# Shift layer on Trainium2: tiles loaded by eight transfers over 128 partitions in place of four over 32, and each half tile stored after its own addition

## The chip, the cores and the metric

The kernel runs as one program on one core of a Trainium2 chip. The metric is device time in microseconds (us), the median of several executions. One further execution was taken with the hardware profiler; times inside the program come from that one. The engines are named as the profile names them: PE (matrix multiply), DVE (vector), ACT (scalar), POOL (GpSimd), SP (the engine that here only issues transfers). "SPq" and "ACTq" are rows for issuing a DMA transfer from SP or ACT.

## The reference, cut to what matters

The reference has four residual layers on `x` of shape (8, 384, 32, 32) in float32: a selective-scan (Mamba) layer, a deformable convolution, a second selective-scan layer with an MLP, and the shift layer. Only the last is touched:

```python
    def _L3_conv_ref(x, offset):               # offset: (48, 2), 48 positions of 8 channels each
        ...
        off_round = jnp.round(offset)
        off_int = off_round.astype(jnp.int32)
        disp = _displace(x.reshape(B, P, cpp, h, w), off_int).reshape(B, C, h, w)   # whole-pixel shift, zeros outside
        sub = offset - lax.stop_gradient(off_round)
        ...                                     # 5 x 5 Gaussian centred at the fractional rest, sum 1
        kw = jnp.repeat(kernel, cpp, axis=0)[:, None]
        out = lax.conv_general_dilated(disp, kw, ..., feature_group_count=C, ...)
        return out
    ...
    x = x + _L3_conv_ref(_gn(x), L3_conv_offset)     # _gn: group norm over 32 groups, no affine
```

A shift by whole pixels and a separable Gaussian are one banded 32 x 32 matrix over rows and one over columns, and all 8 channels of a position share them.

## The kernel before, in words

Layers 0 to 2 take the first 8566 us and are the same in both kernels. While layer 2 finishes, its result goes to DRAM twice: by samples, and as `x3s` with shape [384 channels, 32 rows, 8 images x 32 columns] (L612), so that one row of one channel is 1024 contiguous bytes that hold all 8 images.

The shift layer is built by `shift_parts`. It works in 12 tiles (`NM`). A tile `sxr` has 128 partitions, which are 4 positions (`IG`, index n) times 32 rows; each partition holds 8 channels (`CPP`, index k) x 8 images x 32 columns, 8 KB. So a tile is 1 MB. It is worked on in two chunks of half a tile, chunk 2m with channels k = 0 to 3 and chunk 2m + 1 with k = 4 to 7.

For each tile `load(m)` fills `sxr` from `x3s` (L1962), on SP. For each chunk c: `scale(c)` on POOL multiplies by the group norm's factor into `sxa` (L1980); `over_y` on PE applies the row matrix (L1990, L1992); `turn` on DVE transposes 32 x 32 blocks (L1996); `over_x` on PE applies the column matrix (L2002); `turn_back` on DVE transposes again (L2009); `add(c)` on POOL adds the result to `sxr` in place (L2014). After the second chunk of a tile the stores of the whole tile are written into the program: 32 of them (L2019), one for each channel of the tile, 32 KB each. The stores go in turn to the queues of ACT and SP; each consists of runs of 128 bytes, because the output lies by images.

`main` is a software pipeline with these steps in each turn i:

```python
            for i in range(-3, nch):
                for k, fn in ((3, scale), (2, over_y), (1, over_x), (2, turn), (1, turn_back), (0, add)):
                    if 0 <= i + k < nch:
                        fn(i + k)
                m = i // 2 + AHEAD
                if i % 2 and AHEAD <= m < NM:
                    load(m)
```

Five tiles (`AHEAD`) are loaded ahead of it; `load(m + 5)` is written behind the stores of tile m. `big` hands out the tiles' space from seven buffers in turn, and `done` gives one back. On POOL, `scale(i + 3)` stands ahead of `add(i)`.

The engines run their instructions in order. A scheduler places the waits between engines. For the transfers of SP and ACT it uses eight completion counters: a transfer is given one of the eight, and before it is issued its queue waits until the transfer that had that counter before has landed. Loads and stores of both queues share the eight.

Of the kernel before, what the change touches and what calls it, by code (L numbers as in the profile page):

```python
# [18 lines left out]
H = W = 32  # L19
# [22 lines left out]
CPP = 8  # L42
NP = C // CPP
IG = P // H
# [58 lines left out]
class Net:  # L103
# [1704 lines left out]
    def shift_parts(self, wp, p2, dap, big, done, src_of, srcs, dst):  # L1808
        nc, ins, nb = self.nc, self.ins, self.nb
# [3 lines left out]
        d = {}  # L1813
# [6 lines left out]
        def bc(name, *shape):  # L1820
            t = big(name)
            n = 1
            for k in shape:
                n *= k
            return t[:, :n]
# [131 lines left out]
        CH = NI * W // 2  # L1957
        def load(m):
            xr = d["xr", m] = bc(f"sxr{m}", NI, W).rearrange("p (i w) -> p i w", w=W)
            for n in range(IG):  # L1960
                c = (m * IG + n) * CPP
                nc.sync.dma_start(  # L1962
                    out=xr[n * H : (n + 1) * H].rearrange("p (k b) w -> p k (b w)", k=CPP),
                    in_=srcs[c : c + CPP].rearrange("k y b -> y k b"),
                )

        def table(c, t):
            m, h = divmod(c, 2)
# [4 lines left out]
        def piece(t, c):  # L1973
            return t[:, c % 2 * NI // 2 : (c % 2 + 1) * NI // 2].rearrange("p i w -> p (i w)")
# [36 lines left out]
        def add(c):  # L2011
            m = c // 2
            x = piece(d["xr", m], c)
            nc.gpsimd.tensor_tensor(x, x, d["zt", c], ALU.add)  # L2014
            if c % 2:
                done(f"sxr{m}")
                for k in range(CPP):
                    for n in range(IG):
                        (nc.sync if n % 2 else nc.scalar).dma_start(  # L2019
                            out=dst[:, (m * IG + n) * CPP + k, :].rearrange("b (y x) -> y b x", x=W),  # L2020
                            in_=d["xr", m][n * H : (n + 1) * H, k * nb : (k + 1) * nb, :],
                        )

        def main():
            nch = 2 * NM
# [8 lines that stand above are left out]
        return d, load_consts, kernels_a, kernels_b, stat_load, stat, norms, load, main  # L2034


# [100 lines left out]
```

## Time and profile before

| | |
|---|---|
| median of 3 executions | 8797.08 us (8791.13 to 8799.9) |
| profiled execution, its own time | 8793.49 us |
| its span, first to last instruction | 8791.7 us |
| mean granted PE clock | 0.909 |
| loads of the shift layer, L1962 | 48 of 256 KB, issued from 8566.2 to 8741.4 us |
| stores of the shift layer, L2019 | 192 on ACT's queue (8593.3 to 8772.2 us), 192 on SP's (8617.4 to 8789.0 us), 32 KB each |
| POOL in it | 24 scalings of 1912 ns, 24 additions of 2346 ns |

The times of rows are counted from the start of the span. The rows of a timeline give the start, the length from the first to the last of a group, the engine, the line, the operation, what is written and read, and how many. A wait row names who waited, for whom, how long in total, how often, and the longest. A DMA row of a window gives the packets, the megabytes and the time of the packets as a share of 16 engines' time in that window; it can pass 100% when packets overlap in an engine.

### The profile page before, as it was taken

The page shows a single profiled execution, that of the slowest core. Times are in us where ns is not written, and L with a number is a line of the kernel's source. Part 1 is how long each engine was busy: PE and PEld are TensorE (multiplying, and loading weights), DVE is VectorE, ACT ScalarE, POOL GpSimd, SP SyncE. Part 2 cuts the span into 40 slices and gives each one's busy share as a digit, 9 for nine tenths or more (in the row PEclk, how much of TensorE's full clock was granted, in tenths as well). Part 3 has the DMA queues.
Part 4 walks back from the last instruction along what each step waited for, and adds up shares of the span by engine and source line. Part 5 has one row for each costly group of instructions (what it writes and reads, how often), then busy time and mean ns, then how long its engine had stood idle before and what let it go on. Part 6 is the DMA issues. An engine that isn't in the chain of part 4 may idle for free. (4 is left out here: it accounts for less than half of the span.)

```text
span 8791.7 us, 91535 instructions
## 1 busy us (share of the span) xinstructions
PE 7389.6 (84%) x29688; PEld 3814.4 (43%) x29688; DVE 7510.6 (85%) x8477; ACT 5818.7 (66%) x9501; POOL 5571.8 (63%) x3383
## 2 busy tenths in 40 slices
PE   7888888788886899999999975788888888888886
PEld 2232233223222788788878861233333333333232
DVE  6999999999996788988898886898898988898872
ACT  6777777777774656665666556676777777776740
POOL 6999999999997000000000007999898989999954
PEclk8899899899887999999999997899889999999988
DMA  4555545555454654464446434566666656666646
GB/s 127 123 127 120 125 116 125 126 122 126 115 126 115 169 141 117 112 165 132 118 125 160 128 85 113 136 149 159 156 148 145 154 139 154 151 150 160 159 135 112
DMA packets 803572, 1179.30 MB, mean 134 GB/s; under 512 B 267042, under 2 KB 419650, under 8 KB 769288
## 3 DMA queue, kind: packets, MB, share of 16 engines
q1 hardware_dynamic: 743780, 1157.20, 53.7%
q10 hardware_dynamic: 57844, 10.06, 0.6%
q0 software_dynamic: 1456, 6.07, 0.2%
q8 instruction: 237, 3.88, 0.2%
q14 instruction: 255, 2.09, 0.1%
HBM read 984.11 MB, written 188.98 MB: 133 GB/s over the span
## 5 line engine op out<-in xcount | busy, mean ns | idle before, releaser
L539 POOL TENSOR_TENSOR db<-dub,bc 128x1024 f32<-128x1024 f32 x1536 | 3608.7, 2359 | 377.5 <-DVE hs L551 166.7
L531 ACT ACTIVATE da<-dtb,vec 128x512 f32<-128x512 f32 x3072 | 2122.1, 691 | 609.2 <-DVE hs L564 410.5
L551 DVE TENSOR_TENSOR_SCAN da<-da,db 128x1024 f32<-128x1024 f32 x960 | 2193.3, 2285 | 129.9 <-ACT da L531 86.9
L472 POOL TENSOR_TENSOR dt<-dt,sp_e 128x512 f32<-128x512 f32 x96 | 122.5, 1276 | 2473.1 <-DMA bc<-bcd 2468.8
L1792 PE MATMUL wacc<-fsm,fxk 128*128 128x195 f32 (+21 forms) x10624 | 1572.4, 306 | 132.5 <-DVE fsm L1755 69.7
L1792 PEld LDWEIGHTS wacc<-fsm,fxk 128*128 128x128 f32 x10624 | 1472.7, 195 | 269.1 <-DVE fsm L1755 141.3
L551 DVE TENSOR_TENSOR_SCAN hs<-da,db 128x1024 f32<-128x1024 f32 x576 | 1315.0, 2283 | 198.2 <-POOL db L524 86.2
L562 POOL TENSOR_TENSOR hs<-hs,bc 128x1024 f32<-128x1024 f32 x576 | 1358.0, 2358 | 33.8 <-ACT st L557 33.8
L564 DVE TENSOR_TENSOR hs<-da,bc 128x1024 f32<-128x1024 f32 x960 | 1175.5, 1224 | 127.9 <-PE y L574 78.6
L574 PE MATMUL y<-hs,cols 128*32 128x512 f32 x6144 | 975.4, 654 | 279.1 <-POOL hs L562 253.7
L1755 DVE TENSOR_TENSOR fsm<-fhy,fhx 128x585 f32<-128x585 f32 (+39 forms) x3136 | 1007.6, 383 | 92.9 <-PE wacc L1792 89.9
L1738 DVE TENSOR_TENSOR fxk<-fxt,fwk 128x1024 f32<-128x1024 f32 (+1 forms) x688 | 809.6, 1177 | 12.2 <-DMA fxt<-fxd 11.4
L1715 ACT ACTIVATE fhy<-fpyx,cell 128x416 f32<-128x416 f32 (+10 forms) x832 | 422.8, 580 | 374.7 <-DVE fsm L1755 374.6
L574 PEld LDWEIGHTS y<-hs,cols 128*32 128x32 f32 x6144 | 191.7, 114 | 1004.1 <-issue 516.1
L651 PE MATMUL ps_m<-hid,wm 128*128 128x512 f32 x1152 | 550.6, 633 | 61.8 <-ACT hid L646 27.8
L632 PE MATMUL ps_h<-t,wm 128*128 128x512 f32 x1152 | 531.1, 605 | 45.0 <-DVE sp_e L464 24.4
L1698 ACT ACTIVATE fhx<-fpyx,cell 128x352 f32<-128x352 f32 (+9 forms) x640 | 344.3, 609 | 237.0 <-DVE fsm L1755 222.8
L364 PE MATMUL ps_in<-xn,winr 128*128 128x512 f32 x576 | 326.8, 714 | 175.0 <-ACT xn L353 127.1
L651 PEld LDWEIGHTS ps_m<-hid,wm 128*128 128x128 f32 x1152 | 227.0, 203 | 394.7 <-issue 283.0
L632 PEld LDWEIGHTS ps_h<-t,wm 128*128 128x128 f32 x1152 | 216.1, 193 | 364.7 <-issue 273.4
L583 PE MATMUL ps_z<-xn,winr 128*128 128x512 f32 x576 | 303.0, 674 | 47.7 <-DVE sp_e L464 47.7
L1720 ACT ACTIVATE fhy<-fhy,cols 128x1184 f32<-128x1184 f32 (+8 forms) x208 | 307.4, 1478 | 6.8
(238 smaller groups left out, 9826.3 us busy)
## 6 DMA issues: line engine op xcount, KB each, us to landing
dtb<-dtd SPq DMA_DIRECT2D x768, 256.0 KB
dub<-dtd SPq DMA_DIRECT2D x768, 256.0 KB
fpyx<-fposd SPq DMA_DIRECT2D x104, 1024.0 KB
fxt<-fxd SPq DMA_DIRECT2D x96, 1024.0 KB
wm<-in_w SPq DMA_DIRECT2D x96, 768.0 KB
bc<-bcd SPq DMA_DIRECT2D x256, 256.0 KB
x<-x SPq DMA_DIRECT2D x73, 768.0 KB
dtd<-dt SPq DMA_DIRECT2D x192, 256.0 KB
```

What stands on the lines that cost most here:

```text
L531: nc.scalar.activation(da[:, i, :], s["dtb", j][:, k, :], AF.Exp, scale=na[:, j, n + i : n + i + 1])
L539: nc.gpsimd.tensor_tensor(db, du, s["bc"][p][:, 0], ALU.mult)
L551: nc.vector.tensor_tensor_scan(h1, da1, db1, 0.0, ALU.mult, ALU.add)
L562: nc.gpsimd.tensor_tensor(s["hs", m], s["hs", m], c, ALU.mult)
L564: nc.vector.tensor_tensor(hs_tile(s, m), s["da", m], c, ALU.mult)
L574: nc.tensor.matmul(s["y"][k * IP : (k + 1) * IP, :], sel, s["hs", p * NSUB + k][:, i, :], start=mlp and p == 0 and i == 0, stop=p == NQP - ...
L632: nc.tensor.matmul(ps, s["w1", q][:, k, f * P : (f + 1) * P], s["t"][:, k, :], start=(k == 0), stop=(k == G - 1))
L651: nc.tensor.matmul(ps, s["w2", q][:, f, o * P : (o + 1) * P], s["hid", q][:, f, :], start=(f == 0), stop=(f == 3))
L1715: nc.scalar.activation(hy[:, at : at + (yb - ya) * W], s["pyx", j][:, 0, ya * W : yb * W], AF.Abs, bias=bias)
L1738: nc.vector.tensor_tensor(t[:, :n], x, wk[:, j : j + 1, :].to_broadcast([P, n, P]), ALU.mult)
L1755: nc.vector.tensor_tensor(self.sub(sm, at, [(r * w, n), (w, r), (1, w)]), self.sub(hy, hy_at[by] + xa, [(r * W, n), (W, r), (1, w)]), self ...
L1792: nc.tensor.matmul(a[:, ya - 4 * o : yb - 4 * o, xa:xb], k, self.sub(sm, sm_at[by], [(w, yb - ya), (1, w)]), start=o not in s["open"], sto ...
```

## The change

A tile is loaded by eight transfers in place of four. Before, a transfer brought one position n: 32 partitions, each with eight rows of 1 KB. Now it brings one channel index k of all four positions: 128 partitions, each with one row of 1 KB, 128 KB. Its source in `x3s` is four blocks (the positions, 256 KB apart) of 32 consecutive rows. The 16 stores for channels k = 0 to 3 are written behind the addition of the first chunk, the 16 for k = 4 to 7 behind that of the second; before, all 32 stood behind the second. All else, the number of stores and bytes included, is as before.

```diff
         def load(m):
             xr = d["xr", m] = bc(f"sxr{m}", NI, W).rearrange("p (i w) -> p i w", w=W)
-            for n in range(IG):
-                c = (m * IG + n) * CPP
-                nc.sync.dma_start(
-                    out=xr[n * H : (n + 1) * H].rearrange("p (k b) w -> p k (b w)", k=CPP),
-                    in_=srcs[c : c + CPP].rearrange("k y b -> y k b"),
-                )
+            c = m * IG * CPP
+            src = srcs[c : c + IG * CPP].rearrange("(n k) y b -> k n y b", k=CPP)
+            for k in range(CPP):
+                nc.sync.dma_start(out=xr[:, k * nb : (k + 1) * nb].rearrange("p b w -> p (b w)"), in_=src[k])
 ...
             nc.gpsimd.tensor_tensor(x, x, d["zt", c], ALU.add)
             if c % 2:
                 done(f"sxr{m}")
-                for k in range(CPP):
-                    for n in range(IG):
-                        (nc.sync if n % 2 else nc.scalar).dma_start(
-                            out=dst[:, (m * IG + n) * CPP + k, :].rearrange("b (y x) -> y b x", x=W),
-                            in_=d["xr", m][n * H : (n + 1) * H, k * nb : (k + 1) * nb, :],
-                        )
+            for k in range(c % 2 * CPP // 2, (c % 2 + 1) * CPP // 2):
+                for n in range(IG):
+                    (nc.sync if n % 2 else nc.scalar).dma_start(
+                        out=dst[:, (m * IG + n) * CPP + k, :].rearrange("b (y x) -> y b x", x=W),
+                        in_=d["xr", m][n * H : (n + 1) * H, k * nb : (k + 1) * nb, :],
+                    )
```

## The prediction, made before the changed kernel ran

> **What bounds the shift layer now.** Only the last 226 us of the span are touched. I read the timeline of SP first, because every load and half of the stores go through it, then POOL's timeline, the chain of waits, and the DMA queues of two windows.
>
> ```profile
> 8566.23 50.72 SPq L1962 DMA_DIRECT2D sxr<-x3s  x20
> 8617.39 9.84 SPq L2019 DMA_DIRECT2D out<-sxr  x16
> 8627.27 5.71 SPq L1962 DMA_DIRECT2D sxr<-x3s  x4
> ...
> 8651.37 9.61 SPq L2019 DMA_DIRECT2D out<-sxr  x16
> 8661.02 8.17 SPq L1962 DMA_DIRECT2D sxr<-x3s  x4
> 8669.29 9.63 SPq L2019 DMA_DIRECT2D out<-sxr  x16
> ...
> 8741.98 47.47 SPq L2019 DMA_DIRECT2D out<-sxr  x80
> ```
>
> SP works in a beat: 16 stores (9.6 us), 4 loads (8.2 us), 17.9 us for a tile. It begins to store only at 8617 and ends last, at 8789.5, with 80 stores in a row. So SP sets the end. POOL doesn't:
>
> ```profile
> 8655.86 1.91 POOL L1980 TENSOR_TENSOR sxa<-sxr,stab 128x1024 f32<-128x1024 f32 x1 [9.95 <-DMA out<-sxr]
> 8657.73 2.35 POOL L2014 TENSOR_TENSOR sxr<-sxr,szt 128x1024 f32<-128x1024 f32 x1
> 8660.03 1.91 POOL L1980 TENSOR_TENSOR sxa<-sxr,stab 128x1024 f32<-128x1024 f32 x1
> 8661.90 2.35 POOL L2014 TENSOR_TENSOR sxr<-sxr,szt 128x1024 f32<-128x1024 f32 x1
> ```
>
> It has 8.4 us of work for a tile and then idles 9.5 to 10 us. The row blames a store, but a scaling reads what a load brings: tile 6 was issued from 8643.45 to 8651.3 and its scaling starts at 8655.86. (The two share a counter, so the name is the wrong one.) Loads reach POOL late although they stand five tiles ahead, because on SP they stand behind the stores of tile m.
>
> ```profile
> 8593.34 1.59 DMA out<-sxr
> 8594.95 3.05 DMA sxr<-x3s
> ```
>
> Issue to landing is 1.59 us for a store alone, 3.05 us for a 256 KB load. Last, the price of packets. Queue q1 is SP's; these are its rows in the window 8570 to 8582 us (loads alone) and 8776 to 8789 us (stores alone), and the page's totals:
>
> ```profile
> q1 hardware_dynamic: 2483, 2.40, 113.0%
> ...
> q1 hardware_dynamic: 7089, 0.86, 41.0%
> ...
> DMA packets 803572, 1179.30 MB, mean 134 GB/s; under 512 B 267042, under 2 KB 419650, under 8 KB 769288
> q1 hardware_dynamic: 743780, 1157.20, 53.7%
> q10 hardware_dynamic: 57844, 10.06, 0.6%
> ```
>
> A load's 1 KB packet takes 1.13 x 16 x 12 us / 2483 = 87 ns there, 200 GB/s in all. A store's 128 B packet takes 0.41 x 16 x 13 us / 7089 = 12 ns. In the trace's packet records the 1 KB packets have a lower quartile of 46 ns, and from 8627 to 8742 us a mean of 65 ns.
>
> **The change, part by part.** The built order of the changed program keeps POOL, PE, DVE and ACT as they were, instruction for instruction. SP gets 96 loads for 48 and the same 192 stores: 24 issues for a tile instead of 20. The step is about 0.5 us an issue (16 stores in 9.6 us, SP's issue row 449 ns), so 2 us more for a tile. One load is moved past stores: the first of tile 5 now stands ahead of tile 0's on SP.
>
> *Stores by halves.* I cost this at nothing. ACT's first store already goes at 8593.34, when the first addition (8590.96 + 2.35) ends, and the second addition starts only at 8600: each store waits for its own half already. And SP's stores run tiles behind the additions (the first at 8617 for an addition done at 8593). That lag is the cover; if it were gone, a half tile's POOL time, 4.3 us, would be gained once. A loss by it could come only through the counters, below.
>
> *The loads: on how many DMA engines?* This decides everything. Every shift transfer of the trace runs on 16 engines. [...] a transfer's engines are the largest number up to 16 that divides the outermost dimension (not of size 1) of both access patterns[...]. Each engine used sends one 4-byte packet at the end, so the trace can be asked: the rule, summed over all issues (18 rows give 9 engines, 50 give 10, 98 give 14), yields 56,600 on SP's queue and 3,706 on ACT's; the packet records hold exactly 56,600 and 3,706 (the few loads of 4-byte rows counted in; 16 for every transfer would be 57,064 and 3,716). But in each of these both patterns have suitable outer sizes. The new load has 128 partitions on one side and, in the built program, [4 positions, 32 rows, 256] on the other, for the positions aren't adjacent. By the rule that is 4 engines. By the nearest row (all present loads) it is 16, and 128 KB would be 8 packets to an engine, some 0.4 us. [...] I take the rule, since it missed none of 60,306 packets.
>
> Price of one load, L, by packet: 32 x 46 ns = 1.47 us if the four engines never meet; 32 x 87 ns = 2.8 us if two always share. [...] I take the stage's mean of 65 ns, L = 2.08 us; both ends stay in the range. Eight loads of a tile then need 16.6 us on the same four engines, where the four loads take some 5 us (1 MB at 200 GB/s) on sixteen.
>
> *Opening.* The built order gives the loads of tiles 0 to 4 (and the first of tile 5) all eight counters in strict turn, with no store between; today ACT's first store waits only for tile 0's load. Now SP's first store, its 42nd transfer, waits for tile 4's third load, the 35th, and ACT's for the 34th. First load packet at 8568.8 (packet records): 8568.8 + 35 x 2.08 + 0.5 landing = 8642 for SP's first store (now 8617). [...] lands at 8568.8 + 41 x 2.08 + 0.5 = 8654.6. SP's fifth store waits for it: 8655, and 12 stores x 0.5 later, 8661, tile 0 is stored (now 8627.3). Lost: 34 us. POOL's early scalings (tile 4's now at 8619.9) slip too, but are ahead of this.
>
> *Beat.* With a tile's first load issued at t, load j lands at t + 0.9 + 0.5 + jL: 1.4 us is the 3.05 of a load less its 16 packets (1.4) with a little rounding. Loads 6 to 8 wait for counters of loads 1 to 3, the next tile's first stores for loads 4 and 5, and the fifth store for the first, which stands behind all eight loads: t + 1.4 + 16.6 + 0.3. Then 12 stores: 24.3 us for 17.9. ACT waits with it, having handed counters to these loads. POOL's 8.4 us and ACT's 16 x 0.5 us fit within. Seven beats, less the one load already counted: 170 - 2 = 168 us, where SP now takes 114.7 us (8627.3 to 8742.0) and 9.5 for tile 7's stores, a fifth of its last row.
>
> *Tail.* From there 4 tiles x 16 stores remain, 64 x 0.5 = 32 us, and 2 us to the end. Sum: 8661 + 168 + 32 + 2 = 8863, against a span of 8791.7: +71 us. The profiled execution took 8793.49, 1.8 over its span and 3.6 under the median of 8797.08; I add the difference to the median: 8868 us.
>
> **Ends.** With 46 ns (and 1.5 us a beat for ACT's stores, which the mean of 65 ns holds already: half of 16 x 16 x 12 ns): store 0 ends at 8637, beat 21, 7 x 21 - 1.5, tail 34: 8817, +25, so 8822. With 87 ns: 8690, beat 30.1, 7 x 30.1 - 2.8, tail 34: 8932, +140, so 8937.
>
> **Rivals.**
> *Sixteen engines after all (faster).* Place: SP's queue in the beat. Eight loads of 128 partitions land 2 us after issue, and nothing waits but the issuing: 192 stores + 56 loads at 0.5 us = 124 us from 8594 (first addition), some 10 us of leftover waits and 2 us for the end: 8730, -62 us, 8735. For it: [...] the exact count of 4-byte packets never tried an outer 4 against 128. [...] The point of decision: with L = 1 us (8 engines) the same sum gives opening 8617, beat 17.2, end about 8770; it meets the present span near L = 1.15, seven engines.
> *Four engines that don't meet.* The end of 46 ns, 8822. For it: [...] 46 ns is the median of the stage. [...]
> *Neither.* The loads keep their 200 GB/s, and only 4 issues x 0.5 us are added for a tile, 14 us over seven beats, taken back by earlier first halves: near 8800.
>
> **Chances.** About 0.2% (18 us) is what this measurement can tell from no change. Four engines meeting in part: 0.52 (8840 to 8960); four engines not meeting: 0.26 (8800 to 8840); sixteen: 0.13; neither: 0.06; worse than 8960: 0.03. Slower by over 0.2% (above 8815): 0.79; within: 0.07; faster: 0.14. The range 8800 to 8960 leaves out sixteen engines and the worst, and about half of "neither": a little under 0.2. Nearly all of the chance is on one side.
>
> **What would show it.** Right: q1's packets fall by 384 to 743,396 (96 loads x 4 end packets for 48 x 16); with sixteen engines they rise to 744,548. SP's first store near 8642; the beat 21 to 30 us; in the opening a DMA share near a quarter with 50 to 90 GB/s, where it is full with 200. Waits of POOL at L1978 grow. Wrong, if the loads' window shows over 200 GB/s, SP's first store comes before 8600 and its beat is 12 to 13 us.

## The result, and the profile after

The changed kernel takes 8818.76 us (median of 10 executions, 8816.32 to 8824.0) where the kernel before takes 8795.81 us (10 executions in turn with it, 8787.18 to 8799.9). The ratio is 1.0028, 95% interval 1.002 to 1.0037: slower by 23 us. The forecast was 8868 us: the direction and the main mechanism (four engines) hold, but the loss is a third of the forecast one, and it lies where the rival "four engines that don't meet" put it (8822). The profiled execution took 8821.17 us over a span of 8819.4 us, at a granted clock of 0.908 against 0.909 before, so the clock plays no part.

The timeline of SP, after (start, length, what it issued):

```profile
8567.25 56.55 SPq L1963 DMA_DIRECT2D sxr<-x3s  x41
8623.91 13.47 SPq L2017 DMA_DIRECT2D out<-sxr  x16
8637.42 6.18 SPq L1963 DMA_DIRECT2D sxr<-x3s  x7
...
8657.17 7.49 SPq L1963 DMA_DIRECT2D sxr<-x3s  x8
8666.19 11.71 SPq L2017 DMA_DIRECT2D out<-sxr  x16
8677.95 7.79 SPq L1963 DMA_DIRECT2D sxr<-x3s  x8
...
8771.97 45.20 SPq L2017 DMA_DIRECT2D out<-sxr  x80
```

SP begins to store at 8623.9 (before: 8617.4), its beat is 20.8 to 21.7 us (before: 17.9), and it still ends last. Against the rows of before, the two spans differ by 27.7 us. Tile 0 is stored 10.1 us later (8637.4 for 8627.3; 1.0 us of it, because the stage starts that much later in this execution). From there to the last row (six beats and the loads of a seventh) it takes 134.6 us where it took 114.7: 19.9 us. From the last row to the end it is 2.3 us shorter.

SP's queue in the window 8570 to 8582 us (loads alone), then 8804 to 8817 us (stores alone), then over the whole page:

```profile
q1 hardware_dynamic: 1063, 1.06, 26.4%
...
q1 hardware_dynamic: 7237, 0.87, 41.8%
...
q1 hardware_dynamic: 743396, 1157.20, 53.2%
```

SP's queue has 743,396 packets, the number that the prediction gave for four engines. The loads fill 26.4% of sixteen engines, that is about four (25% would be exact), and move 89 GB/s in place of 200. A packet takes 0.264 x 16 x 12 us / 1063 = 47.7 ns there. In the packet records the 1 KB packets have a median of 46 ns and a mean of 48.1 ns from 8627 to 8742 us, where before had 65.

The chain of work that ended last shows the opening load by load (start, length):

```profile
8585.75 1.38 SPq L1963
8587.18 1.38 SPq L1963
...
8595.64 1.82 SPq L1963
8597.50 1.38 SPq L1963
```

Eight rows stand from 8585.75 up to 8597.50, each one load: 11.75 us, 1.47 us a load, which is 32 packets of 46 ns. The counters do not hold SP here. The load issued at 8575.50 landed at 8583.95 by the counter's own record, and the next load with its counter is issued only at 8587.18; from 8576 to 8622 us SP has no wait for a DMA. It is the issue itself that lasts 1.3 to 1.8 us, where before has 0.30 to 0.45 once its opening is under way. So the pace is that of the four engines, and SP's issuing is held to it; how it is held, the records do not tell. POOL (its timeline, and its waits: us in total, times, longest) runs at that pace too:

```profile
8594.39 1.91 POOL L1978 TENSOR_TENSOR sxa<-sxr,stab 128x1024 f32<-128x1024 f32 x1 [3.96 <-DMA sxr<-x3s]
8596.26 2.34 POOL L2012 TENSOR_TENSOR sxr<-sxr,szt 128x1024 f32<-128x1024 f32 x1
8600.27 1.91 POOL L1978 TENSOR_TENSOR sxa<-sxr,stab 128x1024 f32<-128x1024 f32 x1 [1.66 <-DMA sxr<-x3s]
...
POOL sxa L1978 <- DMA sxr<-x3s: 78.9, 13, 11.1
```

A scaling starts every 5.88 us, that is four loads of 1.47 us: half a tile. In before, the profile put POOL's waits at this line down to stores (74.1 us), which the prediction argued to be the wrong name. Here it puts 78.9 us down to loads and 25.5 to stores.

### The profile page after: what moved, and what is told of

Same layout as the page of the kernel before. It is cut to its first block, busy times and chain, and to the rows that moved or that the text cites. A ratio compares the mean times of both kernels' runs of the same rounds, so it can differ in the third digit from the quotient of the medians.

```text
span 8819.4 us, 91611 instructions
## 1 busy us (share of the span) xinstructions
PE 7399.1 (84%) x29688; PEld 3819.8 (43%) x29688; DVE 7503.8 (85%) x8477; ACT 5817.8 (66%) x9501; POOL 5572.0 (63%) x3383
## 3 DMA queue, kind: packets, MB, share of 16 engines
q1 hardware_dynamic: 743396, 1157.20, 53.2%
## 5 line engine op out<-in xcount | busy, mean ns | idle before, releaser
L651 PE MATMUL ps_m<-hid,wm 128*128 128x512 f32 x1152 | 550.9, 633 | 61.7 <-ACT hid L646 27.7
L583 PE MATMUL ps_z<-xn,winr 128*128 128x512 f32 x576 | 302.9, 674 | 47.7 <-DVE sp_e L464 47.7
```

The source lines that it names most:

```text
L651: nc.tensor.matmul(ps, s["w2", q][:, f, o * P : (o + 1) * P], s["hid", q][:, f, :], start=(f == 0), stop=(f == 3))
```

## The experiments

Theory F: the loss is the four engines, 8 x 1.47 us of loads for a tile ahead of the stores on the same engines. Rival I: it is the added issues (20 in the opening, 4 in a beat, 0.5 us each). Rival S: it is the stores by halves, through the order of the counters. All ratios are to the kernel before, on the same chip.

**One half of the change at a time.** The first kernel takes the new `load` and keeps the old stores:

```diff
-            for n in range(IG):
-                nc.sync.dma_start(out=xr[n * H : (n + 1) * H]..., in_=srcs[c : c + CPP]...)
+            for k in range(CPP):
+                nc.sync.dma_start(out=xr[:, k * nb : (k + 1) * nb]..., in_=src[k])
```

> The eight loads over 128 partitions alone; the 32 stores of a tile stay behind the second addition, as before. Theory F (four engines): a load of 128 KB runs on four DMA engines, 32 packets x 46 ns = 1.47 us of them, eight of them 11.8 us of a tile's beat, and this makes the whole loss: slower by 20 to 28 us (ratio 1.0023 to 1.0032), beat of SP near 21 us, first store of SP near 8624. Rival I (issues: 20 more in the opening, 4 more in a beat, 0.5 us each) expects the same here. Rival S (it is the stores by halves, which change whose counter waits for whom): no change, beat 17.9 us.

Measured: 8819.5 us, ratio 1.0028 (1.0018 to 1.0039), q1's packets 743,396. SP's timeline:

```profile
8567.78 56.32 SPq L1963 DMA_DIRECT2D sxr<-x3s  x41
8624.21 13.45 SPq L2017 DMA_DIRECT2D out<-sxr  x16
8637.70 6.20 SPq L1963 DMA_DIRECT2D sxr<-x3s  x7
```

It is the changed kernel over again, row for row within 1.2 us. The second kernel keeps the old `load` and takes the new stores:

```diff
             if c % 2:
                 done(f"sxr{m}")
-                for k in range(CPP):
+            for k in range(c % 2 * CPP // 2, (c % 2 + 1) * CPP // 2):
```

> The stores by halves alone; the four loads over 32 partitions as before. Theory F: each store already waited for its own half only, and SP's stores run tiles behind: within 5 us of before (ratio 0.9994 to 1.0006), beat 17.9 us. Rival I: the same. Rival S: slower by 15 to 25 us. A third way: the halves shorten the loop that holds the beat today (load landing, scaling, addition, ACT's stores, next load), and the gain was hidden in the changed kernel by the loads: faster by some us.

Measured: 8792.72 us, ratio 1.0001 (0.9992 to 1.0009), with the rows of before. So the loads make the whole loss, and the halves make nothing either way. S falls; F and I remain.

**The same issues and bytes on sixteen engines.** Each load takes one position and half of its channels:

```diff
-            for k in range(CPP):
-                nc.sync.dma_start(out=xr[:, k * nb : (k + 1) * nb]..., in_=src[k])
+            for k in range(0, CPP, CPP // 2):
+                for n in range(IG):
+                    c = (m * IG + n) * CPP + k
+                    nc.sync.dma_start(out=xr[n * H : (n + 1) * H, k * nb : (k + CPP // 2) * nb]...,
+                                      in_=srcs[c : c + CPP // 2].rearrange("k y b -> y k b"))
```

> As the changed kernel, but each of the eight loads of 128 KB takes one position (32 partitions, outermost dimension 32) and half of its channels: as many issues of as many bytes, on sixteen engines. Theory F: the loss goes; a load is 8 packets an engine, 0.4 to 0.7 us, so SP's beat is no longer set by them: not slower than before, ratio 0.993 to 1.000, q1's packets 744,548. Rival I (issues): as the changed kernel, ratio 1.0028. If the price were the 32 partitions and not the engines, the opening would still move 200 GB/s.

Measured: 8794.65 us, ratio 1.0003 (0.9995 to 1.0011), q1's packets 744,548. The loss is gone with as many issues as the changed kernel has: rival I falls. Why there is no gain either is looked at two experiments on.

**128 partitions, with the source in one, eight or two runs.** In three kernels only the choice of source rows differs from the changed kernel, so the order of all instructions and the counter of every transfer are those of the changed kernel, by the trace. (The rows come from other channels than the tables belong to, so these kernels leave out the right assignment, as the expectations say.) First, 128 rows that lie together:

```diff
-            src = srcs[c : c + IG * CPP].rearrange("(n k) y b -> k n y b", k=CPP)
+            src = srcs[c : c + IG * CPP].rearrange("(k n) y b -> k (n y) b", k=CPP)
```

> As the changed kernel, but each load reads 128 rows that lie next to each other in x3s (channels are assigned to positions in another order than the tables and stores have, so the output is a permuted mixture): 128 partitions, 128 KB, eight issues, and the source merges into one dimension of 128. Theory F: sixteen engines; L falls from 1.47 us to some 0.4 to 0.6 us, the opening's window shows over 200 GB/s [...], and the time is the forecast of sixteen engines, 8735, ratio 0.992 to 0.996. Rival I: ratio 1.0028. q1's packets 744,548 under F.

Measured: 8734.3 us, ratio 0.9934 (0.9921 to 0.9948), q1's packets 744,548. Then eight runs of 16 rows:

```diff
-            src = srcs[c : c + IG * CPP].rearrange("(n k) y b -> k n y b", k=CPP)
+            src = srcs[c : c + IG * CPP].rearrange("c (h y) b -> (c h) y b", h=2)
...
-                nc.sync.dma_start(out=xr[:, k * nb : (k + 1) * nb]..., in_=src[k])
+                nc.sync.dma_start(out=xr[:, k * nb : (k + 1) * nb]..., in_=src[k : k + 50 : 7])
```

> As the changed kernel in the same order, but each load reads eight runs of 16 rows of x3s, so the outermost dimension is 8 (the output is a mixture of rows; some rows are read twice and some not at all). Theory F: L = 16 x 46 ns = 0.74 us; by the prediction's sum the first store of SP comes at 8568.8 + 26 + 0.5 = 8595, tile 0 is stored at 8606, beat 1.4 + 5.9 + 0.3 + 6 + 1.5 = 15.1 us, end 8606 + 105 + 34 = 8745: ratio 0.993 to 0.996, between the changed kernel and the run on sixteen engines. q1's packets 743,396 + 384 = 743,780. Rival I: 1.0028. [...]

Measured: 8752.98 us, ratio 0.9955 (0.994 to 0.9971), q1's packets 743,780. Last, two runs of 64 rows:

```diff
-            src = srcs[c : c + IG * CPP].rearrange("(n k) y b -> k n y b", k=CPP)
+            src = srcs[c : c + IG * CPP].rearrange("(n k j) y b -> k n (j y) b", n=2, j=2)
```

> As the changed kernel, instruction for instruction in the same order, but each load of 128 KB reads two runs of 64 rows of x3s (channels assigned to positions in another order than the tables and stores have: the output is a permuted mixture), so the outermost dimension is 2. Theory F (engines = the outermost dimension, 46 ns a packet): L = 64 x 46 ns = 2.94 us. By the prediction's own sum with this L: SP's first store 8568.8 + 35 x 2.94 + 0.5 = 8672, tile 0 stored at 8696, beat 1.4 + 23.5 + 0.3 + 6 + 1.5 = 32.7 us, end 8696 + 7 x 32.7 - 3 + 34 = 8956: ratio 1.018. q1's packets 743,396 - 192 = 743,204. Rival I (issues): as the changed kernel, 1.0028. If the loss were the jumps between runs in DRAM, two long runs would be cheaper than four.

Measured: 8958.81 us, ratio 1.0191 (1.0175 to 1.0206), q1's packets 743,204. The loads' window, 8570 to 8582 us, for sixteen, eight and two engines in turn (packets, MB, share of sixteen engines):

```profile
q1 hardware_dynamic: 3455, 3.15, 84.7%
```

```profile
q1 hardware_dynamic: 2209, 2.13, 54.1%
```

```profile
q1 hardware_dynamic: 534, 0.54, 13.5%
```

The shares of the last two stand near eight and two engines of sixteen (50 and 12.5% would be exact), and a packet takes about the same in all three: share x 16 x 12 us / packets is 47.1, 47.0 and 48.5 ns, with the 4-byte packets counted in. In the packet records the 1 KB packets alone have a median of 46 ns in each, and means of 52, 49 and 49. It is not the number of runs in DRAM that costs: two runs cost most (ratio 1.0191) and eight (0.9955) cost less than four (1.0028). Beside the changed kernel's 26.4%, this is F's dose and answer:

| engines | L by 46 ns | span forecast by the prediction's sum | span measured | ratio |
|---|---|---|---|---|
| 2 | 2.94 us | 8956 | 8956.9 | 1.0191 |
| 4 (changed kernel) | 1.47 us | 8817 | 8819.4 | 1.0028 |
| 8 | 0.74 us | 8745 | 8751.4 | 0.9955 |
| 16 | 0.37 us, less than an issue | 8730 (its rival's sum, by issues) | 8732.5 | 0.9934 |

With sixteen engines the loads no longer set the pace: 41 loads take 20.64 us, one per 0.5 us, which is SP issuing.

```profile
8565.19 20.64 SPq L1963 DMA_DIRECT2D sxr<-x3s  x41
8591.76 8.98 SPq L2017 DMA_DIRECT2D out<-sxr  x16
8600.79 3.31 SPq L1963 DMA_DIRECT2D sxr<-x3s  x7
```

**Why sixteen engines over 32 partitions gain nothing.** That kernel and the one with adjacent rows have the same issues, bytes and engines, and lie 60 us apart. SP's waits, first of the kernel with 32 partitions, then of that with adjacent rows:

```profile
SPq L2020 <- DMA out<-sxr: 41.2, 27, 4.3
SPq L1963 <- DMA out<-sxr: 31.4, 17, 14.0
```

```profile
SPq L2017 <- DMA out<-sxr: 11.3, 16, 2.3
...
SPq L1963 <- DMA out<-sxr: 1.8, 4, 0.6
```

With 32 partitions all of the 31.4 us stand in the opening, where loads wait for counters that ACT's stores hold (one of these waits 14.0 us, 17.2 in before); with adjacent rows it is 1.8 us. In the beat of the 32-partition kernel, from 8621 to 8745 us, SP's loads don't wait, but its stores do: 33.6 us for stores and 12.5 for loads.

The trace names the counter of each transfer, and the two kernels hand the counters out differently. With 32 partitions SP's third store of a tile needs the counter of one of ACT's stores two tiles on; that store needs its addition, which on POOL stands behind the scaling of the tile loaded just before; and SP's next loads stand behind its stores. One turn reads: scaling of tile 5 at 8636.0 us, addition for tile 3 done at 8640.3, SP's third store of tile 1 at 8642.3, loads of tile 6 from 8649.6, their scaling at 8654.2. In before a load of tile m + 5 itself needs the counter of one of ACT's stores of tile m + 3, and from 8617 to 8741 us such loads wait 41.7 us. Either way this is a loop over one tile: load landing, scaling, addition, ACT's stores, next load. With adjacent rows (and in the changed kernel) the counters come from ACT's stores that are one or two tiles older, so the loop reaches further back. The loads' window also differs, 215 GB/s at 80 ns for a 1 KB packet against 263 GB/s at 52 ns (means of the packet records). The runs do not separate the two, so how much of the 60 us is the counters and how much the packets stays open.

**The loads off SP.** If before's beat is that loop, loads with other counters break it. The kernel before, with

```diff
-                nc.sync.dma_start(
+                nc.gpsimd.dma_start(
...
-                m = i // 2 + AHEAD
+                m = i // 2 + AHEAD - 1
```

> The kernel before with its four loads of 256 KB issued by POOL in place of SP, and from tile 5 on one half beat later in the order (load m + 5 behind the additions of tile m + 1, so that POOL does not wait for stores just issued). The reading of before: the beat of 17.9 us is a loop through the counters that loads share with ACT's stores (load landing, scaling, addition, ACT's stores, next load), and nothing in it is full: POOL has 8.4 us of work, SP 16 x 0.5. With counters of their own the loads leave the loop: beat 12 to 13 us, set by POOL (8.4 + 4 issues x 0.75 us, as the issues at L1222 cost), end some 40 to 60 us earlier: ratio 0.993 to 0.996. [...] Second rival: issuing and waiting on POOL take what is gained: 0.999 to 1.003.

(What the expectation calls half a beat is one tile in the order.) Measured: 8742.61 us, ratio 0.9944 (0.993 to 0.9957), the fastest of the kernels here that leave nothing of the computation out. POOL's timeline:

```profile
8630.08 2.34 POOL L1962 DMA_DIRECT2D sxr<-x3s  x4
8632.43 1.92 POOL L1980 TENSOR_TENSOR sxa<-sxr,stab 128x1024 f32<-128x1024 f32 x1
8634.30 2.35 POOL L2014 TENSOR_TENSOR sxr<-sxr,szt 128x1024 f32<-128x1024 f32 x1
8636.61 1.91 POOL L1980 TENSOR_TENSOR sxa<-sxr,stab 128x1024 f32<-128x1024 f32 x1
8638.48 2.34 POOL L2014 TENSOR_TENSOR sxr<-sxr,szt 128x1024 f32<-128x1024 f32 x1
8640.77 2.34 POOL L1962 DMA_DIRECT2D sxr<-x3s  x4
```

SP's timeline now has stores alone:

```profile
8604.03 134.36 SPq L2019 DMA_DIRECT2D out<-sxr  x192
```

POOL's beat is 10.7 us, without a gap: 8.4 us of work and four issues of 0.59 us. The 9.5 to 10 us of idling per tile that before showed are gone, and PE, too, is busy all the time from 8600 to 8712 us. The beat no longer sets the end: the last addition ends at 8719.6 us, and SP issues its stores, 0.70 us each, until 8738.4. A control moves the order alone:

> The kernel before with only the order moved: load m + 5 behind the additions of tile m + 1, all loads on SP. It tells what of the gain with loads on POOL is the order. On SP the load then stands behind one tile's stores more, so it comes later for scaling: the loop load, scaling, addition, stores is as long, ratio 0.999 to 1.006. If the order were the gain: 0.994 to 0.996.

Measured: 8790.88 us, ratio 0.9999 (0.999 to 1.0007). So the gain is the other queue, not the later place in the order. That queue has its own counters, it takes the loads out from behind SP's stores, and it moves larger packets (below); the runs do not separate these three.

**The changed kernel's loads on POOL**, by the same two edits made to it:

> The changed kernel with its eight loads of 128 KB over 128 partitions issued by POOL, the same half beat later. Theory F with the same rule on POOL's queue: the loads leave SP's order, [...] 17.9 us a tile, so near before (ratio 0.998 to 1.002), and its opening loads at under 90 GB/s. If the rule does not hold on POOL's queue (16 engines), the time is as of the four loads on POOL or a little above (8 issues): 0.993 to 0.997. Rival I: 1.00 or slower by POOL's 8 issues of 0.75 us: POOL 14.4 us a tile, still under 17.9.

Measured: 8762.84 us, ratio 0.9968 (0.9956 to 0.998). It is the second outcome: on POOL's queue the outermost dimension of 4 does not leave this pattern with four engines. (By the author's estimate these would have carried, for a tile, 8 x 1.47 us of loads and 8192 x 12 ns / 16 = 6.1 us of stores, 17.9 us.) The loads' window:

```profile
q0 software_dynamic: 2031, 1.92, 96.4%
```

The loads now keep all sixteen engines busy, with the very access pattern that SP's queue runs on four. They move 160 GB/s, less than the 215 of the 32-partition loads on POOL. Its stage has a beat of 13.7 us, which is POOL's 8.4 us and eight issues of 0.68, less small overlaps.

**Three tries to improve on it.** The loads of tiles 0 to 4 back on SP, the others on POOL (`(nc.sync if m < AHEAD else nc.gpsimd)`):

> The kernel before with the loads of tiles 0 to 4 on SP as before and those of tiles 5 to 11 on POOL, half a beat later in the order. In the run with all loads on POOL the beat is 10.7 us, but the opening has 20 issues on POOL ahead of the first scaling, and the first addition starts at 8601.7 in place of 8591. Theory: with the opening back on SP the first addition returns to 8591, the beat stays 10.7 us, and the time falls by a further 8 to 11 us: ratio 0.9925 to 0.994. Rival: the opening's loads wait for counters of ACT's stores as before (SP's first store at 8617), SP then runs tiles behind and its 16 x 0.5 us in a beat of 10.7 leave it 2.7 us to catch up: no gain over all loads on POOL, 0.994 to 0.996.

Measured: 8750.72 us, ratio 0.9953 (0.9939 to 0.9966). The first addition is back at 8591.3, but the rival was right. SP's timeline and waits:

```profile
8566.51 55.12 SPq L1962 DMA_DIRECT2D sxr<-x3s  x20
8621.73 124.58 SPq L2019 DMA_DIRECT2D out<-sxr  x192
...
SPq L1962 <- DMA out<-sxr: 39.5, 7, 17.2
```

The opening's loads stand 39.5 us on counters that ACT's stores hold, SP starts to store at 8621.7, and its 192 stores, 0.65 us each now, set the end. The same with the stores by halves:

> The same with the changed kernel's stores by halves. The prediction costed the halves at nothing because SP ran tiles behind the additions, and said that without this cover a half tile's POOL time, 4.3 us, is gained once. Where SP keeps up with the additions, the end comes up to 4 us earlier than in the run with whole tiles (ratio 0.0002 to 0.0005 lower). If SP still lags, the two are equal. If the halves cost by the counters, it is slower.

Measured: 8749.37 us, ratio 0.9952 (0.9938 to 0.9966): equal, since SP still lags (it starts at 8620.4). What the halves give where SP keeps up with the additions was therefore not tried alone. Last, four tiles ahead, eight opening loads on SP and eight on POOL, stores by halves:

> Four loads of 256 KB over 32 partitions (sixteen engines) for each tile: tiles 0 and 1 by SP, which takes eight issues and so each counter once, all others by POOL, two of them ahead of the first scaling; four tiles ahead in place of five; stores by halves. Against the run with all loads on POOL (20 issues ahead of the first scaling, first addition 8601.7, SP's first store 8604): POOL issues 8 loads, 4.7 us from 8567, before the tables it waits for anyway (8579), so the first addition is back at 8591, beat 10.7 us as there: 10 us earlier, and the halves give up to 4 us at the end where SP keeps up: span near 8728, ratio 0.992 to 0.9935. Rival: SP's and ACT's stores are no longer ahead of time to spare (16 x 0.65 us = 10.4 in a beat of 10.7), and what the opening gives is lost in their queues: 0.994 to 0.9955.

Measured: 8746.94 us, ratio 0.9947 (0.9934 to 0.9961): a miss, and not told apart from all loads on POOL. POOL's timeline shows what failed in the opening:

```profile
8571.06 4.68 POOL L1962 DMA_DIRECT2D sxr<-x3s  x8 [91.92 <-DVE smv L1903]
8589.63 3.78 POOL L1980 TENSOR_TENSOR sxa<-sxr,stab 128x1024 f32<-128x1024 f32 x2 [13.89 <-DMA sxr<-x3s]
```

The loads of tiles 2 and 3, issued by POOL at once, share the engines with those of tile 0, whose scaling waits for its load to 8589.6 in place of 8579 (some 4 us of it, because the stage starts that much later in this execution). Later, a load with one tile less of lead lands just too late: seven of the scalings wait 1.3 to 2.8 us for it. The stores' queues, the place that the expectation's rival named, end last: SP's 192 stores, 0.73 us each, run from 8605.3 to 8745.3 us, where the last addition ends at 8733.7.

## Why the prediction was right and wrong, point by point

- *SP sets the end.* Right: the issue of its last store ends at 8817.2, of a span of 8819.4.
- *Stores by halves cost nothing, because SP lags.* Right on the cost: ratio 1.0001 for the halves alone. That the lag is the reason was not tried alone.
- *Four DMA engines, by the outermost dimension of both patterns.* Right. The nearest row of the trace (all loads on sixteen) would have given a gain of 62 us; the rule, borne out by the count of 4-byte packets, decided the sign. In before, sixteen for each transfer would be 57,064 on SP's queue. The records hold 56,600: 464 fewer, which is what 9, 12, 10 and 14 packets make for its transfers of 18, 24, 50 and 98 rows (44, 2, 22 and 8 of them), the largest divisors up to 16. The loads with an outermost 2, 4, 8 and 128 bear it out on SP's queue: 743,204, 743,396, 743,780 and 744,548 packets, which is 2, 4, 8 and 16 of 4 bytes a load, and 13.5, 26.4, 54.1 and 84.7% of sixteen engines. In the changed kernel the load issued at 8575.50 us lands 8.45 us later, five to six times its own 1.47 us, so several loads are on their way at once, and they share the four; which four these are, the records do not tell. It does not hold for the one pattern tried on POOL's queue (96.4%).
- *Price of one load, L = 2.08 us from a mean packet of 65 ns.* This is the step that failed. L is 1.47 us, 32 packets of 46 ns, the lower end that the prediction had worked out; the packets' mean in the beats is 48.1 ns. The mean of 65 ns was taken over from a stage where sixteen engines write into 32 partitions; it belonged to that pattern (in the loads' window, on sixteen engines, a 1 KB packet has a mean of 80 ns over 32 partitions and of 52 over 128). (The burst's 87 ns had the 4-byte packets counted in; its 1 KB packets alone have a mean of 91.) That four engines would meet in part was the author's estimate. No run here shows such a meeting for four engines, or for eight (a mean of 48.4 ns from 8627 to 8742 us). Why they do not meet is not settled: the records do not name a packet's engine.
- *Opening.* With 2.08 us the prediction had SP's first store at 8642; with 1.47 it is 8621, and the trace has 8623.9. The wait there was not the one named: the 35th load had landed at 8622.2, and SP was still issuing its 41st load until 8623.8. Tile 0 stored: 8661 and 8636 by the two, 8637.4 measured.
- *Beat.* 24.3 us by 2.08, 21 by 1.47 and 21.1 measured over the five whole beats from 8657.2 to 8762.9. Of the 44 us by which the span was missed, the seven beats carry 24 (143.6 us to the end of tile 7's stores, in place of 168) and the opening 24; the tail gives 4 back. The sum was sound in the main: with L put right it meets the spans of 2, 4 and 8 engines within 1 to 6 us. One small term doesn't come out of its own numbers: 3.05 us less sixteen packets of 87 ns leaves 1.65 us and not 1.4, which is 2 us over seven beats.
- *Tail.* A little short: 34 us forecast from the end of tile 7's stores, 38.4 measured, because a store took 0.56 us and not 0.5.
- *The crossing point.* The prediction put no change at L = 1.15 us. A straight line between the runs with eight and with four engines (8751.4 at 0.74 us, 8819.4 at 1.47) crosses the span of before at 1.17.
- *Rivals.* Sixteen engines: 8735 forecast, and 8734.3 when the source allows them. Added issues alone ("neither"): no loss that can be measured, 1.0003. Four engines that don't meet: this is what happened, 8822 against 8818.76, at a chance of 0.26 against 0.52 for meeting in part. The median of the stage, 46 ns, was in hand as the evidence for it; a mean of 65 ns that mixes such packets with slower ones (the upper quartile is 72 ns) was weighed above it.

## What to carry to other kernels

Before a transfer is reshaped to span more partitions, look at the outermost dimension on both sides: on SP's queue here the source's 4 set four engines, and the share of the DMA rows (26.4%) shows it at a glance. A packet's time is to be taken from the records of a like pattern, and as the undisturbed value with its quartiles; a mean over a stage with slower packets in it (65 ns there, 46 here) does not carry over. Where two queues share completion counters, ask which transfer held a load's counter before: taking the loads to a queue with counters of its own gained 48 us here, where the order alone gained nothing that can be measured (how much of it is the counters stays open).

## What the runs showed of the hardware that was not expected

- The same load of 128 partitions from four runs, on four engines when SP issues it, keeps sixteen busy when POOL does (26.4% and 96.4% of sixteen).
- On POOL's queue these loads go in larger packets. From the changed kernel to its copy with the loads on POOL, the page's packets of 512 B to 2 KB fall by 12,288 (96 loads x 128 rows of 1 KB) and those of 2 to 8 KB rise by 3072, so there is one packet for four 1 KB rows (in the loads' window 463 of them carry nearly all of the 1.92 MB). Landing was later: for 256 KB at least 4.0 us from issue and 6.2 at the median, where SP's load took 3.05.
- In the opening, SP's 41 loads of 128 KB took 20.64 us to issue on sixteen engines, 56.55 on four and 114.99 on two (0.50, 1.38 and 2.80 us each), though with four the counter that it needed had been free for 3.2 us: issuing fell back to the engines' pace (from 8585.75 to 8597.50 us, 1.47 us from one issue to the next, as 32 packets of 46 ns).
- An issue cost POOL 0.59 us for 256 KB over 32 partitions and 0.68 us for 128 KB over 128, where other transfers of this kernel (L1222) cost it 0.75.
- Loads over 128 partitions on sixteen engines took 263 GB/s (adjacent rows), at which rate SP's issuing is the limit (128 KB in 0.5 us). Over 32 partitions on sixteen engines they took 200 GB/s in before and 215 in the kernel with eight such loads to a tile, both by SP, and 215 on POOL's queue.
